# Layer 0 of a four-layer graph network: T2 of the first piece summed by transfers, T1's self-loops on GpSimd, the second half's row statistics on ScalarE

## The chip, the cores and the metric

One core of a Trainium2 chip runs the whole network in one launch. The metric is the device time in microseconds (us); the times shown are a median over runs, and one further execution was profiled.

## The reference

`x` is 2708 x 512 and `adj` 2708 x 2708, both float32. Four layers each take a row-wise layer norm and relu of `x`, multiply by a normalized adjacency, project with a 512 x 512 weight and add the result to `x`. The change lies in layer 0:

```
h = jnp.maximum(_layernorm(x, axis=-1), 0.0)
deg = jnp.sum(adj_matrix, axis=1)
dinv = (deg + 1.0) ** (-0.5)
aug = dinv[:, None] * (adj_matrix + jnp.eye(n, dtype=adj_matrix.dtype)) * dinv[None, :]
x = x + jax.nn.relu(aug @ h @ weight)
```

So layer 0 needs the column-summed degrees, the norm statistics (mean and variance of each row of `x`) and the aggregation with self-loops (the `eye`).

## The kernel before, in words

**Two levels of seven products.** The nodes are cut into 4 quarters of 677 = 5 x 128 + 37. The 5 full tiles of each quarter go through a two-level Strassen-like scheme, the remaining rows through `tails`. At the outer level the features and nodes of `h` form four parts: XA and XB (first half of the nodes, left and right 256 columns) and XC and XD (second half). The adjacency is four quarters y11, y12, y21, y22, each of 2 x 2 blocks of 128 x 5 x 339 float32 (867,840 bytes, shown as 847.5 KB) and two pieces u of 339 columns. Outer product p multiplies a part of `h` by a block sum:

- 1: XA by y11; 2: XC by y21; 3: XC by y22
- 7: XA by T3 = y22 + y12 + I; 6: XA by T2 = T3 + y11 + I
- 4: XD by T4 = T2 + y21; 5: XB by T1 = y12 + y11 + I

XA, XB, XC are overwritten between products (XA becomes XA - XB, then -XD - XA). Below, "p6(1)" is outer product 6 of piece u = 1. In layer 0 the order is p1(0), p1(1), p7(0), p7(1), p6(1), p2(1), p4(1), p6(0), p2(0), p4(0), the tails of two quarters, p5(0), p5(1), two more tails, an epilogue of projections, then p3.

**One outer product of one piece** (`multiply`) is seven inner products of 5 float32 matmuls each, which the trace shows as 10 records, 2.86 us together. Their order on TensorE is pa (factor 1), pb (6), pa again (2), pc (7), pd (5), pc again (4), pd again (3). VectorE makes the sums of blocks (`inner_y`: t1, t2, t4 and, in layer 0, a t3 in a place of its own) and of `h` (`inner_x`), and empties the PSUM banks: pd's second group is accumulated on top of the first, so it may start only after VectorE has read the first one. ScalarE copies pa to `v` before pa's second group.

**Blocks and queues.** 7 block places lie in `obuf`, 3 in `ends` (named `more`), and some early ones in `h` and `agg`. `free` hands them out; a load into a place waits until its last reader is done. Loads go through SP's DMA queue. Stores of block sums to DRAM (`keep_o`, tensors `osum`, read again by the later layers) and accumulating loads go through GpSimd's (POOL's) queue. Each engine works its queue in order. A scheduler decides the order on each engine; `tc.issue_after(i)` keeps instructions behind i.

**Layer 0 before the change.** T3, T2 and T4 are sums on VectorE. `second_sums(0)` makes T2 of the piece u = 0 right after p1(1) and stores it; it is loaded again for p6(0). T1 is a load of y12 on SP's queue and an accumulating load of y11 on POOL's (L697), then `add_loops` on VectorE (L410, three small instructions a block), then a store. The second half's rows of `x` are loaded into `h` (L238) after T3's sums have left that space; `first_stats` takes bn_stats and bn_aggr on VectorE (L202, L203) for 12 tiles; `other_degrees` sums columns, and after its second call `first_h` takes roots and writes the normalized `h` tile by tile on ScalarE (L221). p6(1) needs XA minus XD, and so this.

Of the kernel before, what the change touches and what calls it, by code (L numbers as in the profile page):

```python
# [8 lines left out]
FP = mybir.dt.float32  # L9
# [3 lines left out]
P = 128  # L13
# [8 lines left out]
U = 2  # L22
# [15 lines left out]
def gnn_kernel(  # L38
# [161 lines left out]
    def stats(src, mv):  # L200
        st = small.tile([P, nc.vector.BN_STATS_DIM], FP, tag="st", name="st")
        nc.vector.bn_stats(st, src)  # L202
        nc.vector.bn_aggr(mv, st)  # L203
# [13 lines left out]
        )  # L217
        return b

    def normalized(t, src, scale, shift):  # L220
        nc.scalar.activation(h[:, t, :], src, AF.Relu, bias=shift, scale=scale)  # L221

    def groups(ts):

# [17 lines left out]
    def first_stats(ts):  # L242
        for t in ts:
            stats(h[:, t, :], mv0[:, t, :])

# [68 lines left out]
    def other_degrees(u, ys):  # L314

        if u == 0:
            parts[1, 1] = upool.tile([P, W], FP, tag="s", name="row")
        for b, blocks in ((0, (ys[1], ys[2])), (1, (ys[7],))):
            ps = ps_out.tile([P, W], FP, tag="out", name="dg_ps")
            tl = tail_place(b, u)  # L320
            column_sums(ps, [tl[:, 0], tl[:, 1]], blocks, parts[b, u])
        if u < U - 1:
            return
# [15 lines left out]
    def first_h(columns, looped):  # L339

        ts = list(columns)
        n, t0 = len(ts), ts[0]
        span = slice(t0, t0 + n)
        pd = ps_sm.tile([P, NT], FP, tag="sm", name="pd")
        for s, t in enumerate(ts):
            nc.tensor.matmul(
                pd[:, s : s + 1], columns[t], ones[:, 0:1], start=True, stop=True
            )
        if looped:
            nc.vector.tensor_copy(deg[:, t0 : t0 + looped], pd[:, :looped])  # L350
        if looped < n:
            nc.vector.tensor_scalar(
                deg[:, t0 + looped : t0 + n], pd[:, looped:n], 1.0, None, ALU.add
            )
        rsqrt(dinv[:, span], deg[:, span], n)
        mv = mv0[:, span, :]
        rstd = rstd_of(mv, n)
        nc.vector.tensor_mul(rstd[:, :n], rstd[:, :n], dinv[:, span])
        sh = shift_of(mv, rstd, n)
        for s, t in enumerate(ts):  # L360
            normalized(t, h[:, t, :], rstd[:, s : s + 1], sh[:, s : s + 1])

    def other_roots():

# [39 lines left out]
    def add_loops(blk, u, times):  # L404

        for k in range(KT):
            lo, hi = max(k * P, u * W), min((k + 1) * P, (u + 1) * W)
            if lo < hi:
                o = blk[:, k, lo - u * W : hi - u * W]
                nc.vector.scalar_tensor_tensor(  # L410
                    o, ident[:, lo - k * P : hi - k * P], float(times), o, ALU.mult, ALU.add
                )

    def by_halves(f, *xs):

# [48 lines left out]
            multiply(xs_, inner_y(blks, u, loops), u, dests)  # L464
            free.extend(blks)

    def multiply(xs_, ys, u, dests):


        cu = slice(u * W, (u + 1) * W)  # L470
# [9 lines left out]
        def bank(name):  # L480
            return ps_agg.tile([P, W], FP, tag="agg", name=name)
# [29 lines left out]
        product(pc, 7, True)  # L511
        u3 = upool.tile([P, W], FP, tag="u3", name="u3")
        at_u3.append(nc.vector.tensor_add(u3, u2, pc).ins)  # L513
        pd = bank("pd")
        product(pd, 5, True)
        give(1, 1, pd, u3, ALU.subtract)
# [56 lines left out]
    def first_part_of_both():  # L573
        nc.scalar.copy(agg[:, 0, 1], agg[:, 0, 0])
# [31 lines left out]
    def first_aggregate(epilogue):  # L606
# [42 lines left out]
        def second_sums(u):  # L649
            for (a, b), t2, y in zip(QUAD, blks[u], t3[u]):  # L650
                nc.vector.tensor_add(t2, t2, y)
                keep_o(t2, "t2", a, b, u)

        for (a, b), blk, y in zip(QUAD, t3[0], temps):
            load_plain("y22", a, b, 0, blk)
            load_plain("y12", a, b, 0, y)
# [2 lines left out]
        for (a, b), y in zip(QUAD, temps):  # L659
            load_plain("y12", a, b, 1, y)  # L660
        multiply(xs_, ys, 1, [p1])
        second_sums(0)
        by_halves(nc.vector.tensor_sub, XA, XA, XB)
        xs_ = inner_x(XA)
        ys = inner_y(t3[0], 0, 0, own_t3)
# [8 lines left out]
        ys = inner_y(t3[1], 1, 0, own_t3)  # L674
        with tc.issue_after(at_u3[-1]):
            second_sums(1)
        with tc.issue_after(at_end[-1]):
            first_stats(range(half, NT))
        other_degrees(1, ys)
        multiply(xs_, ys, 1, [p7])  # L680
        first_part_of_both()
        by_halves(minus_sum, XA, XD, XA)
        free += t3[0][:2] + t3[1]

        def among(places):

            for k, f in enumerate(free):
                if any(f is e for e in places):
                    return free.pop(k)
            return free.pop(0)  # L690


        def first_sums(u, places):
            t1 = [among(places) for _ in QUAD]
            for (a, b), blk in zip(QUAD, t1):
                load_plain("y12", a, b, u, blk)
                nc.gpsimd.dma_start(blk, yb[a, b, u], accum_op=ALU.add)  # L697
            with tc.issue_after(at_u3[-1]):
                for (a, b), blk in zip(QUAD, t1):
                    if a == b:  # L700
                        add_loops(blk, u, OUTER[5][2])
                    keep_o(blk, "t1", a, b, u)
            return t1

        for u in reversed(range(U)):
            if u == 1:
                t2 = blks[1]
            else:
                t2 = [among(in_obuf) for _ in QUAD]
                for (a, b), blk in zip(QUAD, t2):  # L710
                    nc.sync.dma_start(blk, osum["t2", a, b, u])
            xs_ = inner_x(XA)
            multiply(xs_, inner_y(t2, u, 0, own_t3), u, [(0, 1, "added")])
            if u == 1:
                other_roots()
                nc.vector.tensor_sub(XB, XB, XD)
            y21 = [among(more) for _ in QUAD]
            for (a, b), blk in zip(QUAD, y21):
                load_plain("y21", a, b, u, blk)
            xs_ = inner_x(XC)  # L720
            multiply(xs_, inner_y(y21, u, 0, own_t3), u, [(0, 0, "added")])
            for (a, b), t4, y in zip(QUAD, t2, y21):
                nc.vector.tensor_add(t4, t4, y)
                keep_o(t4, "t4", a, b, u)
            free += y21
            if u == 0:
                rows = [tail_rows(True, q) for q in (0, 1)]
            xs_ = inner_x(XD)
            multiply(xs_, inner_y(t2, u, 0, own_t3), u, [(1, 0, "as it is")])
            if u == 0:  # L730
                t1 = first_sums(0, more)
            free += t2
        nc.vector.tensor_add(XC, XC, XA)
        tails(True, (0, 1), rows)
        ends_of_sums()
# [402 lines left out]
```

## Time and profile before

| | us |
|---|---|
| median of 3 runs | 2145.58 (2144.49 to 2147.9) |
| the profiled execution's own time | 2147.35 |
| its span | 2145.6 |
| TensorE busy | 2068.6 (96%) |
| VectorE / ScalarE / GpSimd busy | 1438.6 / 384.7 / 173.7 |
| mean granted TensorE clock | 0.989 of full speed |

The span runs from the first to the last instruction. PE is TensorE, DVE VectorE, ACT ScalarE, POOL GpSimd, SP the queue of SyncE. A line number names the line of the kernel that issues the instruction; a helper such as `multiply` gives all its matmuls one line (L475). Layer 0 up to its first epilogue takes the first 374 us of the span; the rest of the program is not touched by the change.

### The profile page before, as it was taken

What the parts mean: (1) busy time and instruction counts of PE and PEld (TensorE: products, weight loads), DVE (VectorE), ACT (ScalarE), POOL (GpSimd) and SP (SyncE); (2) the same over time, 40 slices, a digit from 0 to 9 for tenths busy, and PEclk for the clock granted to TensorE, in tenths of its full rate; (3) what the DMA queues carried; (4) which work ended last, traced back from release to release, by engine and by line L of the source; (5) the groups of instructions that cost most, each with busy time, mean ns of one, the idle gap of its engine ahead of it and who ended that gap; (6) DMA issues with size and microseconds to landing.
All of it is one profiled execution on the core that took longest, in us unless ns stands there. A gap on an engine that the chain in (4) does not pass through costs nothing.

```text
span 2145.6 us, 19944 instructions
## 1 busy us (share of the span) xinstructions
PE 2068.6 (96%) x7310; PEld 1289.0 (60%) x7310; DVE 1438.6 (67%) x2513; ACT 384.7 (18%) x755; POOL 173.7 (8%) x319
## 2 busy tenths in 40 slices
PE   5989979999999999999999999999999999999998
PEld 2555646556666645566664546666677666666664
DVE  3888847667666867777576879968537755666512
ACT  1111000222000010100001121000116534444401
POOL 0000010211000020200001130000001000000001
PEclk9999989999999999999999999999999999999999
DMA  9884695446454443644453656544541233233212
GB/s 351 346 336 154 191 281 189 161 153 211 164 177 167 148 165 137 234 164 156 162 183 123 218 196 211 176 156 156 192 166 72 96 101 103 91 101 100 80 41 64
DMA packets 78720, 358.05 MB, mean 167 GB/s; under 512 B 10540, under 2 KB 14508, under 8 KB 78624
## 3 DMA queue, kind: packets, MB, share of 16 engines
q1 hardware_dynamic: 51104, 250.98, 34.3%
q0 software_dynamic: 27520, 105.82, 14.6%
q8 instruction: 57, 0.93, 0.2%
q14 instruction: 39, 0.32, 0.0%
HBM read 294.61 MB, written 62.15 MB: 166 GB/s over the span
## 4 chain that ended last, share of the span: by engine, by line
PE 62%; issue 20%; DMA 8%; DVE 7%; POOL 2%; ACT 1%; SPq 0%; POOLq 0%; DVEq 0%; ACTq 0%
PE pa L475 13%; PE pc L475 12%; PE pd L475 12%; PE po L754 7%; PE pb L475 6%; PE pe L1045 4%; PE pt L526 3%; PE pg L893 3%; DMA obuf<-in_yb_dram 2%; DMA h<-in_x_dram 1%; PE pt L531 1%; DVE ends L846 1%; POOL ends L761 1%; DMA ends<-xs 1%; DMA osumt<-obuf 1%
## 5 line engine op out<-in xcount | busy, mean ns | idle before, releaser
L1045 PE MATMUL pe<-obuf,h 128*128 128x339 f32 x1280 | 372.9, 448 | 0.0
L475 PE MATMUL pa<-obuf,h 128*128 128x339 f32 x1050 | 324.0, 454 | 13.4 <-DVE h L420 8.5
L1045 PEld LDWEIGHTS pe<-obuf,h 128*128 128x128 f32 x1280 | 241.2, 189 | 126.4 <-issue 10.0
L754 PE MATMUL po<-ends,agg 128*128 128x512 f32 x640 | 281.4, 596 | 2.1 <-ACT ends L774 1.9
L475 PEld LDWEIGHTS pa<-obuf,h 128*128 128x128 f32 x1050 | 200.1, 192 | 121.4 <-issue 9.4
L754 PEld LDWEIGHTS po<-ends,agg 128*128 128x128 f32 x640 | 119.8, 190 | 144.8 <-issue 137.3
L475 PE MATMUL pd<-obuf,s 128*128 128x339 f32 x550 | 169.0, 454 | 13.3 <-DVE agg L492 13.3
L475 PE MATMUL pc<-t,h 128*128 128x339 f32 x560 | 173.8, 457 | 4.4 <-DVE u L513 4.4
L966 ACT ACTIVATE e<-r,nsr 128x339 f32<-128x339 f32 x352 | 170.7, 566 | 28.6 <-DVE obuf L970 11.7
L475 PE MATMUL pb<-t,s 128*128 128x339 f32 x560 | 169.3, 448 | 0.1
L475 PE MATMUL pd<-t,s 128*128 128x339 f32 x560 | 169.2, 448 | 0.0
L503 ACT COPY v<-pa 128x339 f32<-128x339 f32 x56 | 24.6, 440 | 758.4 <-PE pa L475 738.8
L475 PEld LDWEIGHTS pd<-obuf,s 128*128 128x128 f32 x550 | 105.6, 192 | 68.0 <-DVE agg L492 14.3
L475 PEld LDWEIGHTS pc<-t,h 128*128 128x128 f32 x560 | 108.1, 194 | 60.9 <-DVE u L513 6.0
L475 PEld LDWEIGHTS pd<-t,s 128*128 128x128 f32 x560 | 106.0, 189 | 54.2 <-issue 0.5
L475 PEld LDWEIGHTS pb<-t,s 128*128 128x128 f32 x560 | 105.7, 189 | 54.6 <-DVE s L420 0.7
L475 PE MATMUL pc<-obuf,s 128*128 128x339 f32 x450 | 136.1, 448 | 0.0
L475 PEld LDWEIGHTS pc<-obuf,s 128*128 128x128 f32 x450 | 85.3, 189 | 43.6 <-issue 0.5
L450 DVE TENSOR_TENSOR t<-obuf,t 128x1695 f32<-128x1695 f32 x55 | 105.4, 1917 | 0.0
L780 POOL DMA_DIRECT2D xs<-ends x66 | 35.9, 544 | 817.6 <-DVE ends L779 764.8
L451 DVE TENSOR_TENSOR t<-obuf,t 128x1695 f32<-128x1695 f32 x53 | 101.6, 1917 | 0.0
L449 DVE TENSOR_TENSOR t<-obuf 128x1695 f32<-128x1695 f32 x49 | 94.1, 1920 | 9.8 <-DMA obuf<-in_yb_dram 6.6
(247 smaller groups left out, 2184.2 us busy)
## 6 DMA issues: line engine op xcount, KB each, us to landing
obuf<-in_yb_dram SPq DMA_DIRECT2D x131, 847.5 KB, 4.6
obuf<-osumt SPq DMA_DIRECT2D x100, 847.5 KB, 4.5
osumt<-obuf POOLq DMA_DIRECT2D x23, 847.5 KB, 9.0
xs<-ends POOLq DMA_DIRECT2D x66, 256.0 KB, 2.3
ends<-xs POOLq DMA_DIRECT2D x66, 256.0 KB, 3.4
obuf<-in_yt_dram SPq DMA_DIRECT2D x32, 339.0 KB, 3.6
h<-in_yb_dram SPq DMA_DIRECT2D x11, 847.5 KB, 10.0
ends<-in_yb_dram SPq DMA_DIRECT2D x11, 847.5 KB, 6.2
```

Source lines behind the costliest of these rows:

```text
L449: nc.vector.tensor_add(t1, o12, o11)
L450: nc.vector.tensor_add(t2, o22, t1)
L451: at_t4.append(nc.vector.tensor_add(t4, o21, t2).ins)
L475: nc.tensor.matmul(ps, xs_[q][:, k, :], ys[q][:, k, :], start=start and k == 0, stop=k == KT - 1, skip_group_check=not start,)
L503: nc.scalar.copy(v, pa)
L526: nc.tensor.matmul(ps[c], h[:, NF, c * P : (c + 1) * P], tl[:, 0, :], start=start, stop=False)
L531: nc.tensor.matmul(ps[c], h[g, NF + 1, c * P : (c + 1) * P], tl[g, 1, :], start=False, stop=True)
L754: nc.tensor.matmul(po, cs[c], w_sb[:, c, :], start=(c == 0), stop=(c == NC - 1))
L780: nc.gpsimd.dma_start(xs[t], xt)
L893: nc.tensor.matmul(pk, cs[c], wg_sb[:, c, k, :], start=(c == 0), stop=(c == NC - 1))
L966: nc.scalar.activation(e[:, k], row, AF.Exp, bias=nsr[:, t, s : s + 1], scale=1.0)
L1045: nc.tensor.matmul(pe[c], h[:, t, c * P : (c + 1) * P], a, start=(t == 0), stop=False)
```

## The change

- `second_sums(0)` is gone. T2 of u = 0 is made later, in two calls of `second_sums_later` during p2(1) and p4(1): load the stored T3 block, accumulate y11 onto it by a transfer from POOL's queue, add the self-loops of the two diagonal blocks on GpSimd, store.
- T1 takes the same path (`accumulated`): its self-loops move from VectorE to GpSimd, and its blocks are taken in the order (0,0), (0,1), (1,1), (1,0).
- `other_stats` replaces `first_stats` for the second half: two passes of 12 activations of 128 x 512 on ScalarE with an accumulated output (Identity for the sum, Square of mean minus x for the variance), each followed by one small scaling on VectorE.
- `first_h` for the second half is called inside p7(1), ahead of its pd, and not ahead of p7(1)'s first matmul in the program; `normalized` writes half rows (128 x 256), for the second half the right columns (XD) first.
- The copy of agg[:, 0, 0] to agg[:, 0, 1] is a transfer on POOL's queue, no more a ScalarE copy.
- T4's sums and stores stand behind u3 of p6 of the same piece.

```
+    def other_stats(ts):
+        span = slice(ts.start, ts.stop)
+        y = ytp.tile([P, 2, W], FP, tag="yt", name="y").rearrange("p s w -> p (s w)")[:, 0:D]
+        for s, f, mean in ((0, AF.Identity, None), (1, AF.Square, mv0)):
+            for t in ts:
+                nc.scalar.activation(
+                    y, h[:, t, :], f,
+                    bias=0.0 if mean is None else mean[:, t, 0:1],
+                    scale=1.0 if mean is None else -1.0,
+                    accum_out=mv0[:, t, s : s + 1],
+                )
+            nc.vector.tensor_scalar(mv0[:, span, s], mv0[:, span, s], 1.0 / D, None, ALU.mult)
...
-        for s, t in enumerate(ts):
-            normalized(t, h[:, t, :], rstd[:, s : s + 1], sh[:, s : s + 1])
+        fs = slice(0, D // 2), slice(D // 2, D)
+        for f in fs if t0 < half else fs[::-1]:
+            for s, t in enumerate(ts):
+                normalized(t, h[:, t, :], rstd[:, s : s + 1], sh[:, s : s + 1], f)
...
+        def accumulated(blks, key, a_b, u, load):
+            for a, b in a_b:
+                blk = blks[a, b]
+                load(blk, a, b)
+                nc.gpsimd.dma_start(blk, yb[a, b, u], accum_op=ALU.add)
+                if a == b:
+                    add_loops(blk, u, 1, nc.gpsimd)
+                keep_o(blk, key, a, b, u)
...
-        second_sums(0)
...
-        with tc.issue_after(at_end[-1]):
-            first_stats(range(half, NT))
+        other_stats(range(half, NT))
         other_degrees(1, ys)
-        multiply(xs_, ys, 1, [p7])
-        first_part_of_both()
+        multiply(xs_, ys, 1, [p7], other_h)
+        nc.gpsimd.dma_start(agg[:, 0, 1], agg[:, 0, 0])
...
         def first_sums(u, places):
-            t1 = [among(places) for _ in QUAD]
-            for (a, b), blk in zip(QUAD, t1):
-                load_plain("y12", a, b, u, blk)
-                nc.gpsimd.dma_start(blk, yb[a, b, u], accum_op=ALU.add)
-            with tc.issue_after(at_u3[-1]):
-                for (a, b), blk in zip(QUAD, t1):
-                    if a == b:
-                        add_loops(blk, u, OUTER[5][2])
-                    keep_o(blk, "t1", a, b, u)
-            return t1
+            t1 = {ab: among(places) for ab in QUAD}
+            accumulated(
+                t1, "t1", ((0, 0), (0, 1), (1, 1), (1, 0)), u,
+                lambda blk, a, b: load_plain("y12", a, b, u, blk),
+            )
+            return [t1[ab] for ab in QUAD]
+        t2 = {}
+        def second_sums_later(a_b):
+            for ab in a_b:
+                t2[ab] = among(in_obuf)
+            accumulated(
+                t2, "t2", a_b, 0, lambda blk, a, b: nc.sync.dma_start(blk, osum["t3", a, b, 0])
+            )
         for u in reversed(range(U)):
...
+            u3_of_6 = at_u3[-1]
...
+            if u == 1:
+                second_sums_later(QUAD[:2])
             xs_ = inner_x(XC)
             multiply(xs_, inner_y(y21, u, 0, own_t3), u, [(0, 0, "added")])
-            for (a, b), t4, y in zip(QUAD, t2, y21):
-                nc.vector.tensor_add(t4, t4, y)
-                keep_o(t4, "t4", a, b, u)
+            with tc.issue_after(u3_of_6):
+                for (a, b), t4, y in zip(QUAD, ops, y21):
+                    nc.vector.tensor_add(t4, t4, y)
+                    keep_o(t4, "t4", a, b, u)
             free += y21
-            if u == 0:
+            if u == 1:
+                second_sums_later(QUAD[2:])
+            else:
                 rows = [tail_rows(True, q) for q in (0, 1)]
...
```

More of the change, by code (lines that the diff above doesn't have):

```diff
@@ L218, in shift_of, with normalized @@
         return b
-    def normalized(t, src, scale, shift):
-        nc.scalar.activation(h[:, t, :], src, AF.Relu, bias=shift, scale=scale)
+    def normalized(t, src, scale, shift, fs=slice(0, D)):
+        nc.scalar.activation(h[:, t, fs], src[:, fs], AF.Relu, bias=shift, scale=scale)
     def groups(ts):
@@ L321, in other_degrees, with other_h @@
             column_sums(ps, [tl[:, 0], tl[:, 1]], blocks, parts[b, u])
-        if u < U - 1:
-            return
+    def other_h():
         columns = {}
@@ L402, in load_plain, with add_loops @@
         nc.sync.dma_start(blk, yb[j + a, i + b, u])
-    def add_loops(blk, u, times):
+    def add_loops(blk, u, times, engine=None):
         for k in range(KT):
@@ L409, in add_loops @@
                 o = blk[:, k, lo - u * W : hi - u * W]
-                nc.vector.scalar_tensor_tensor(
-                    o, ident[:, lo - k * P : hi - k * P], float(times), o, ALU.mult, ALU.add
-                )
+                i = ident[:, lo - k * P : hi - k * P]
+                if engine is None:
+                    nc.vector.scalar_tensor_tensor(o, i, float(times), o, ALU.mult, ALU.add)
+                else:
+                    assert times == 1
+                    engine.tensor_tensor(o, o, i, ALU.add)
     def by_halves(f, *xs):
@@ L465, in outer_product, with multiply @@
             free.extend(blks)
-    def multiply(xs_, ys, u, dests):
+    def multiply(xs_, ys, u, dests, beside=None):
         cu = slice(u * W, (u + 1) * W)
@@ L513, in multiply @@
         at_u3.append(nc.vector.tensor_add(u3, u2, pc).ins)
+        if beside is not None:
+            beside()
         pd = bank("pd")
@@ L693, in first_sums @@
         def first_sums(u, places):
-            t1 = [among(places) for _ in QUAD]
-            for (a, b), blk in zip(QUAD, t1):
-                load_plain("y12", a, b, u, blk)
-                nc.gpsimd.dma_start(blk, yb[a, b, u], accum_op=ALU.add)
-            with tc.issue_after(at_u3[-1]):
-                for (a, b), blk in zip(QUAD, t1):
-                    if a == b:
-                        add_loops(blk, u, OUTER[5][2])
-                    keep_o(blk, "t1", a, b, u)
-            return t1
-        for u in reversed(range(U)):
[L706 to L711, printed above, removed]
+            t1 = {ab: among(places) for ab in QUAD}
[11 more added lines that the diff above has]
+            )
+        for u in reversed(range(U)):
+            ops = blks[1] if u == 1 else [t2[ab] for ab in QUAD]
             xs_ = inner_x(XA)
-            multiply(xs_, inner_y(t2, u, 0, own_t3), u, [(0, 1, "added")])
+            multiply(xs_, inner_y(ops, u, 0, own_t3), u, [(0, 1, "added")])
+            u3_of_6 = at_u3[-1]
             if u == 1:
@@ L719, in first_aggregate @@
                 load_plain("y21", a, b, u, blk)
+            if u == 1:
+                second_sums_later(QUAD[:2])
             xs_ = inner_x(XC)
             multiply(xs_, inner_y(y21, u, 0, own_t3), u, [(0, 0, "added")])
-            for (a, b), t4, y in zip(QUAD, t2, y21):
-                nc.vector.tensor_add(t4, t4, y)
-                keep_o(t4, "t4", a, b, u)
+            with tc.issue_after(u3_of_6):
+                for (a, b), t4, y in zip(QUAD, ops, y21):
+                    nc.vector.tensor_add(t4, t4, y)
+                    keep_o(t4, "t4", a, b, u)
             free += y21
-            if u == 0:
+            if u == 1:
+                second_sums_later(QUAD[2:])
+            else:
                 rows = [tail_rows(True, q) for q in (0, 1)]
             xs_ = inner_x(XD)
-            multiply(xs_, inner_y(t2, u, 0, own_t3), u, [(1, 0, "as it is")])
+            multiply(xs_, inner_y(ops, u, 0, own_t3), u, [(1, 0, "as it is")])
             if u == 0:
                 t1 = first_sums(0, more)
-            free += t2
+            free += ops
         nc.vector.tensor_add(XC, XC, XA)
```

## The prediction

> **What bounds the kernel now.** The page first: TensorE is busy for 96% of the span, so only its gaps can be won. The table of stretches shows where layer 0 has them.
>
> ```profile
> PE 2068.6 (96%) x7310; PEld 1289.0 (60%) x7310; DVE 1438.6 (67%) x2513; ACT 384.7 (18%) x755; POOL 173.7 (8%) x319
> ```
>
> ```profile
> core 0: us, PE busy (x) PEld busy (x) DVE busy (x) ACT busy (x) POOL busy (x), PEclk, DMA share, GB/s
> 100.00:125.00 25.00, 23.37 (x103) 13.11 (x101) 21.01 (x22) 4.20 (x5) 2.12 (x4) 1.00 1.02 404
> 125.00:150.00 25.00, 21.58 (x89) 14.23 (x89) 23.84 (x50) 1.80 (x6) 2.67 (x5) 0.92 1.00 382
> 150.00:175.00 25.00, 15.94 (x41) 9.55 (x40) 19.45 (x31) 9.25 (x14) 0.53 (x1) 0.74 0.19 70
> 250.00:275.00 25.00, 25.00 (x89) 16.60 (x88) 23.51 (x24) 0.88 (x2) 2.85 (x4) 1.00 0.98 284
> 275.00:300.00 25.00, 12.74 (x41) 8.13 (x40) 7.00 (x14) 0.44 (x1) 6.95 (x10) 0.79 1.02 281
> ```
>
> PE idles in 125 to 175 (call it the head) and in 275 to 300 (the T1 stage). In both the DMA engines are full just before. The chain of waits says what ends the gaps:
>
> ```profile
> 116.26 22.88 DMA h<-in_x_dram
> ...
> 159.54 3.64 ACT h L221 x5
> 163.20 1.50 DVE h L420
> 164.75 5.71 PE pa L475 x10
> ...
> 280.07 13.98 DMA obuf<-in_yb_dram
> ...
> 295.46 1.83 DVE t L449
> 297.29 0.43 DVE agg L492
> 297.77 5.74 PE pd L475 x10
> ```
>
> Head: rows of x issued at 116.3 land at 139.1; bn_stats, roots and twelve activations follow, and p6(1) starts at 164.75, 8.5 us after p7(1) ended. T1: p4(0)'s last group (pd) could start at 285.4. It waits 12.3 us for a PSUM read on VectorE (L492), which stands behind T1's self-loops (L410), which wait for the accumulating load of block (1,1). POOL's timeline shows these loads (L697):
>
> ```profile
> 247.89 0.91 POOL L697 DMA_DIRECT2D ends<-in_yb_dram  x1 [7.74 <-DMA ends<-in_yb_dram]
> 258.07 0.89 POOL L697 DMA_DIRECT2D ends<-in_yb_dram  x1 [1.03 <-DMA ends<-in_yb_dram]
> 267.59 0.89 POOL L697 DMA_DIRECT2D ends<-in_yb_dram  x1 [8.63 <-DMA ends<-in_yb_dram]
> 279.52 1.80 POOL L697 DMA_DIRECT2D obuf<-in_yb_dram  x2
> ```
>
> **What the Trainium skill says.** (1) "TensorE: Matmul & The Clock Gate", Part 1: after about 3.4 us of idling the array runs at half clock for about as long. The trace agrees: ten matmuls take 5.7 us in place of 2.86 after the gaps of 8.5 and 12.3 us, and 3.1 after one of 1.6. (2) "DMA: Bandwidth & Descriptors", Issuing engines are not separate DMA queues: SP's and POOL's transfers share 16 engines. Agrees: 1.0 busy wherever both have work. (3) "GPSIMD Engine Reference", Elementwise: a two-input add takes some 2.6 cycles an element at 1.2 GHz; 0.28 us for 128 columns. No such row in this trace. (4) "SBUF — State Buffer", Who interferes with whom: a VectorE instruction with two SBUF inputs and a GpSimd instruction that reads SBUF exclude each other. Not shown here.
>
> **Prices.** A plain block is 867,840 bytes at the 420 GB/s that full stretches show (84 to 100 us): 2.07 us of all engines. An accumulating one: from 248.8 to 294.1 the engines moved 9 plain blocks (18.6 us) and 5 accumulating ones; less 1.8 us of latency that leaves 24.9, so 5.0 each. Its quickest landing is 7.5 us, its slowest 17.3. Block add 1.83 us, half-size PSUM read 0.42, activation of 128 x 512 0.71 (12 in 8.56, L221). An activation with accumulated output isn't in the trace: from 0.71 to 1.0, I take 0.75. A half-row activation: from the 339- and 512-column rows (566, 797 ns), 0.36. GpSimd add: 0.28 to 1.0 with dispatch and the port, I take 0.4, and up to 1.83 more behind a VectorE add.
>
> **Head.** Removed: four block adds (7.3 us of VectorE) and four stores (8.3 us of DMA) of T2(0), twelve bn pairs (0.67 each, 8.0 us of VectorE), the 2.46 us ScalarE copy. y22(1) overwrites T2(0)'s places, so its four loads no longer wait for stores: in the changed order of SP's queue they follow y12(1) and start near 83 us, not 99.5. T3(1)'s sums then wait for no transfer; the last read of x's place ends near 105.8 us by adding up VectorE's order, and x is issued at 103 and 106 (before 113.9 and 116.3). Still to move then: one y21 block, three T3 stores, x at 3.1 twice, 14.5 us from 101.3: x lands at 114 to 118, not 134 to 139.
>
> Pass 1 on ScalarE is 12 x 0.75: done near 123. Queued behind it stand the two degree copies and p7(1)'s `v`, which pa's second group needs. p7(0) loses its waits and ends near 118 (before 122.6); degrees take 2; p7(1) starts at 120, and `v` is wanted at 126. So pass 1 has 3 us to spare. Pass 2 waits for its mean on VectorE, behind T2(1)'s adds (to 125), then 9 us and two small ScalarE steps: done near 135. p7(1) ends near 142, with 1.8 us for the twelve column matmuls now ahead of pd. The roots' chain waits in VectorE's order for the reads of pd and pc and for two block adds: scales near 142.5. Then 5 half activations (1.9), -XD - XA (1.4): p6(1) at 146. Its pb waits for XB - XD (2.73) and the second half, to 151.5; six groups of 2.86 and half of a cold start give an end at 170. Before: 188.4. **Gain 18**, range 13 to 20 (low end: 1.0 us an activation; x 5 us later costs up to 3).
>
> The agg transfer (1.39 MB, issued near 120, wanted near 160) lies beside it, and the first half's ten half activations take what five whole ones took (10 x 0.36 to 5 x 0.73): nothing.
>
> **T2(0).** The four loads of T3 stand where four loads of T2 stood; new are four accumulations (20 us of DMA) between 135 and 205, where the engines are half busy, and on POOL they wait behind the bg load (for the column matmuls, 134): nothing. But block (1,1) takes the place of a block that p2(1) reads to its end (191). Load 4.6, POOL 0.9 with an accumulation of 7.5 (quiet DMA, 0.5 in this stretch before), three GpSimd adds 1.2, block add 1.83, PSUM read 0.4: VectorE is through at about +17, where p4(1)'s last group wants it at +17.15. **Cost 1**, from 0 to 6 if the accumulation takes 12. p6(0) reads the sums later; covered.
>
> **T1.** Measured from p2(0)'s start (248.2 before). Before: T4's stores at -16, -14, -9 and +8, accumulations from 0, (1,1) landed at +45.9, PE went on at +49.6. In the changed order all four T4 adds stand behind p6(0)'s last PSUM read, so they end at +2.3, +4.6, +8.0, +10.9, and their stores stand ahead of T1's first accumulation on POOL, now at +11.4. The place for (1,1) still comes free at +20. From +2.9 to its landing the engines move 4 accumulating blocks (20) and 13 plain ones (four T4 stores, four y12, three y12 of u = 1, two T1 stores: 26.9): +52 with latency. One accumulation fewer than before (that of u = 1 falls behind), but T4's stores come in. The wait itself stays: in VectorE's order the t3 of p5(0), a reader of (1,1), still stands ahead of the PSUM read that p4(0)'s last group needs. Then adds 1.2, t3 1.83, read 0.4: PE goes on at +55.5. **Loss 6**, from -15 (whole gap and cold start gone) to +15. What follows, tails and p5, has the same order behind it; T1(1)'s chain would end near +79, p5(1) starts near +98: covered.
>
> **Sum.** -18 + 1 + 6 = -11 on the profiled execution's 2147.35 (span 2145.6 and 1.8 around it): 2136.3. That execution lies 1.8 above the median, so I say **2135** for the median.
>
> **Rivals.**
> - *T1's gap shrinks too.* For it: self-loops leave VectorE, and (1,1)'s accumulation no longer stands behind one of u = 1. Against: DMA share 1.02 in that stage. If PE goes on at +40 to +48: 2114 to 2126. Chance 0.27.
> - *The statistics lose what they win.* ScalarE's 24 activations in front of `v`, or x no earlier: p7(1) stalls, 2138 to 2150. Against: 5 us between landing and bn_stats' end now. Chance 0.10.
> - *Slower: POOL's queue becomes a chain.* Each GpSimd add waits for its accumulation, and stores and the next accumulations wait behind it. If adds are also held up by VectorE's two-input adds (1.83 each, three to six in a row), (1,1) is issued at +48 and more. Against: transfers, not issue, fill the stage. The head's 18 are eaten from a landing at +64 on; at +72 to +80: 2150 to 2163. Chance 0.13.
> - *Likeliest*, the sum: 2126 to 2143. Chance 0.50.
>
> **Numbers.** A measurement of this kernel can tell about 0.2% from no change, 4.3 us. The likeliest case gives 0.44 faster and 0.06 same; the second 0.27 faster; the third 0.02 and 0.08; the fourth 0.13 slower. Together 0.73, 0.14, 0.13. Range 2114 to 2150: it leaves out the slower case and a total of both gaps.
>
> **What would show it.** Right: x's rows land near 116, p7(1) ends near 142, p6(1) near 170, ScalarE's 24 activations under 1 us; in the T1 stage PE still idles at pd of p4(0), for 15 to 20 us, with DMA at 1.0. Wrong: pa's second group in p7(1) waiting for ScalarE; PE without a gap in p4(0); GpSimd adds of several us; p4(1) stopping at its end for over 6 us.

## The result, and the profile after

The changed kernel takes **2170.54 us** (median of 4 runs, 2167.51 to 2171.65) against 2145.03 for the kernel before: a ratio of 1.0117, 95% interval 1.0099 to 1.0136. It is slower by 25 us; the forecast was 2135, and 2150 at most. The profiled execution has a span of 2167.8 us (before 2145.6).

TensorE (PE) runs the same 7310 matmuls. It is busy for 7.5 us more, and idle for 14.7 us more (91.7 us of the span, before 77.0):

```profile
PE 2076.1 (96%) x7310; PEld 1293.2 (60%) x7310; DVE 1422.3 (66%) x2475; ACT 406.2 (19%) x824; POOL 185.0 (9%) x342
```

The starts of the block products in TensorE's timeline say where. Each column is the length of a stage in us, from start to start: "head" from p7(0) to p2(1), "T2" p2(1) and p4(1), "T1" p4(0) and the tails after it, then p5(0). p7(0) itself starts at 97 to 103 us in these profiles; the three latest are e4, e5 and e11. Each row is one profiled execution, beside the median of all runs; the ratio is to runs of the kernel before that were taken with them. From the start of p3 on, where no edit changes anything, these executions took 1735.7 to 1739.5 us, so some 4 us of a span can come from there.

| run | head | T2 | T1 | p5(0) | median us | ratio to before (95%) |
|---|---|---|---|---|---|---|
| before | 90.0 | 40.0 | 51.9 | 20.1 | 2145.0 | |
| after | 91.6 | 51.3 | 60.0 | 21.1 | 2170.5 | 1.0117 (1.0099 to 1.0136) |
| e1: statistics alone | 104.9 | 40.0 | 48.6 | 20.1 | 2161.4 | 1.0076 (1.0057 to 1.0095) |
| e2: after, statistics as before | 78.1 | 51.4 | 59.6 | 21.6 | 2159.6 | 1.0064 (1.0045 to 1.0084) |
| e3: after, T2(0) as before | 104.8 | 40.0 | 59.6 | 22.2 | 2174.1 | 1.0134 (1.0113 to 1.0155) |
| e4: after, T1 and T4 as before | 93.4 | 45.9 | 49.0 | 20.1 | 2153.9 | 1.0045 (1.0032 to 1.0058) |
| e5: T2(0) alone | 79.6 | 46.5 | 52.0 | 20.1 | 2143.4 | 0.9994 (0.9984 to 1.0004) |
| e6: after, accumulations first | 92.1 | 48.5 | 62.2 | 21.3 | 2172.8 | 1.0134 (1.0118 to 1.0149) |
| e7: after, pass 1 behind `v` | 82.5 | 51.4 | 59.6 | 21.3 | 2163.4 | 1.0088 (1.0073 to 1.0103) |
| e8: after, T4 as before | 92.9 | 43.6 | 58.2 | 20.1 | 2162.3 | 1.0087 (1.0066 to 1.0108) |
| e9: after, sums bound | 92.1 | 41.9 | 49.0 | 27.4 | 2162.0 | 1.0083 (1.0064 to 1.0102) |
| e10: after, copy on ScalarE | 85.2 | 51.3 | 60.0 | 21.6 | 2165.5 | 1.0101 (1.0084 to 1.0118) |
| e11: e5 with half rows, early degrees | 79.6 | 44.1 | 48.7 | 20.1 | 2142.0 | 0.9987 (0.9980 to 0.9994) |
| e12: e11, three changes of order | 79.6 | 40.0 | 46.9 | 20.1 | 2133.2 | 0.9946 (0.9931 to 0.9960) |
| e13: e8, p5(0)'s sums bound | 92.7 | 45.6 | 42.3 | 28.2 | 2155.6 | 1.0056 (1.0037 to 1.0075) |
| e14: e12, loops bound | 79.6 | 40.0 | 41.3 | 20.1 | 2130.9 | 0.9939 (0.9920 to 0.9959) |
| **e15: e14, roots first** | 70.9 | 40.0 | 40.8 | 20.1 | **2122.3** | **0.9896 (0.9870 to 0.9922)** |
| e16: e15, loops on GpSimd | 70.6 | 40.0 | 43.2 | 28.3 | 2130.7 | 0.9934 (0.9908 to 0.9959) |

From before to after: start 1.3, head 1.6, T2 11.3, T1 8.0, p5(0) 1.0, and -1.0 in all that follows: 22.2, the difference of the spans. Stretches as in the prediction's table, and 300 to 325 (start and end, then busy time and number of instructions of each engine, TensorE's clock, DMA share, GB/s):

```profile
125.00:150.00 25.00, 10.90 (x32) 6.83 (x31) 5.03 (x15) 16.77 (x45) 0.85 (x2) 0.73 0.58 236
150.00:175.00 25.00, 20.55 (x70) 13.29 (x70) 18.74 (x36) 14.57 (x34) 4.06 (x7) 0.80 0.73 186
275.00:300.00 25.00, 21.88 (x77) 14.20 (x75) 18.16 (x19) 0.88 (x2) 3.86 (x8) 1.00 1.03 341
300.00:325.00 25.00, 11.58 (x23) 6.91 (x24) 11.32 (x12) 0.00 (x0) 6.08 (x12) 0.59 0.90 267
```

The head's gap has moved from 150-175 to 125-150, where PE is busy 10.9 of 25 us, VectorE (DVE) only 5.0 and ScalarE (ACT) 16.8: ScalarE is now what the head waits for. The chain of waits in this stretch (start, length, what):

```profile
106.17 30.17 DMA h<-in_x_dram
...
142.34 0.35 ACT v L523
...
142.73 4.97 PE pa L495 x10
```

ScalarE's timeline shows why `v`, a copy of 0.4 us, comes at 142. Brackets hold the idle time before an instruction and what ended it; L252 is pass 1:

```profile
125.41 0.63 ACT L252 ACTIVATE y<-h 128x512 f32<-128x512 f32 x1 [16.62 <-DMA h<-in_x_dram]
...
136.42 0.63 ACT L252 ACTIVATE y<-h 128x512 f32<-128x512 f32 x1 [7.28 <-DMA h<-in_x_dram]
...
142.23 0.45 ACT L523 COPY v<-pa 128x339 f32<-128x339 f32 x1
```

Pass 1 was issued ahead of `v`, and twice waited for rows of x. PE's other waits, in p4(1) (T2) and p4(0) (T1):

```profile
227.82 4.81 PE L495 MATMUL pc<-t,h 128*128 128x339 f32 x10 [2.26 <-DVE u L533]
236.95 5.65 PE L495 MATMUL pd<-obuf,s 128*128 128x339 f32 x10 [4.32 <-DVE agg L512]
...
302.20 5.45 PE L495 MATMUL pc<-t,h 128*128 128x339 f32 x10 [5.32 <-DVE u L533]
318.87 5.64 PE L495 MATMUL pd<-obuf,s 128*128 128x339 f32 x10 [11.22 <-DVE agg L512]
```

Each is a wait for VectorE, and each restart costs more: the ten matmuls behind it take 4.8 to 5.65 us in place of 2.86. That an array that idled runs slower for a while is what "TensorE: Matmul & The Clock Gate", Part 1, of the Trainium skill says, but the length of idling that it gives, about 3.4 us, does not sort these waits: 2.26 us was enough here, and in e8 the same ten matmuls took 3.12 us after a longer wait:

```profile
228.73 3.12 PE L495 MATMUL pc<-t,h 128*128 128x339 f32 x10 [3.22 <-DVE u L533]
```

What VectorE did in T2, and then POOL's queue there and in T1 (the accumulating loads are L681, the stores L415, the self-loops L432):

```profile
226.32 0.19 DVE L570 TENSOR_TENSOR obuf<-obuf,ident 128x32 f32<-128x32 f32 x1 [6.88 <-DMA obuf<-in_yt_dram]
...
234.55 1.93 DVE L472 TENSOR_TENSOR ends<-obuf 128x1695 f32<-128x1695 f32 x1 [6.05 <-POOL obuf L432]
236.39 0.51 DVE L512 TENSOR_TENSOR agg<-pd,u 128x339 f32<-128x339 f32 x1
```

```profile
202.69 0.53 POOL L415 DMA_DIRECT2D osumt<-obuf  x1 [1.72 <-DVE obuf L757]
211.88 0.90 POOL L681 DMA_DIRECT2D obuf<-in_yb_dram  x1 [8.66 <-DMA obuf<-osumt]
223.56 0.55 POOL L415 DMA_DIRECT2D osumt<-obuf  x1 [10.77 <-DMA obuf<-osumt]
224.09 0.92 POOL L681 DMA_DIRECT2D obuf<-in_yb_dram  x1
233.42 1.09 POOL L432 TENSOR_TENSOR obuf<-obuf,ident 128x128 f32<-128x128 f32 x3 [8.41 <-DMA obuf<-in_yb_dram]
...
300.51 0.94 POOL L681 DMA_DIRECT2D obuf<-in_yb_dram  x1
...
315.30 1.13 POOL L432 TENSOR_TENSOR obuf<-obuf,ident 128x128 f32<-128x128 f32 x3 [8.57 <-DMA obuf<-in_yb_dram]
```

In T2 the adds to the tail rows (L570), which wait for a load of these rows, hold up u3 (L533) until 227, and the sum of p6(0) that needs block (1,1) (L472) holds up the PSUM read (L512) until 236. (1,1)'s accumulation is issued at 224.09, right behind a store that POOL issued at 223.56. In T1 (1,1)'s accumulation has landed at 315.3.

### The profile page after: what moved, and what is told of

Its sections match the earlier page's. It is cut to its first block, busy times and chain, and to the rows that moved or that the text cites. A ratio compares the mean times of both kernels' runs of the same rounds, so it can differ in the third digit from the quotient of the medians.

```text
span 2167.8 us, 20020 instructions
## 1 busy us (share of the span) xinstructions
PE 2076.1 (96%) x7310; PEld 1293.2 (60%) x7310; DVE 1422.3 (66%) x2475; ACT 406.2 (19%) x824; POOL 185.0 (9%) x342
## 4 chain that ended last, share of the span: by engine, by line
PE 41%; issue 41%; DMA 8%; DVE 6%; POOL 3%; ACT 1%; SPq 0%; POOLq 0%; ACTq 0%; DVEq 0%
PE pa L495 9%; PE pd L495 8%; PE pc L495 8%; PE po L790 5%; PE pb L495 4%; PE pg L929 3%; PE pt L548 2%; DMA ends<-in_yb_dram 2%; DMA obuf<-in_yb_dram 2%; DMA h<-in_x_dram 1%; DMA ends<-xs 1%; POOL ends L797 1%; DMA obuf<-osumt 1%; PE pt L553 1%; DVE t L471 1%
## 5 line engine op out<-in xcount | busy, mean ns | idle before, releaser
L495 PE MATMUL pa<-obuf,h 128*128 128x339 f32 x1050 | 327.6, 457 | 21.6 <-ACT v L523 14.3
L495 PEld LDWEIGHTS pc<-obuf,s 128*128 128x128 f32 x450 | 85.2, 189 | 43.7 <-issue 0.5
```

Source lines behind the costliest of these rows:

```text
L495: nc.tensor.matmul(ps, xs_[q][:, k, :], ys[q][:, k, :], start=start and k == 0, stop=k == KT - 1, skip_group_check=not start,)
```

## The experiments

**First the parts.** The change has three: the statistics with half rows and the copy as a transfer; T2(0) by accumulating transfers; T1's loops on GpSimd with T4's sums behind u3. The table of stages suggests that each loses by itself; the rivals say that one cause (the late head, or DMA bandwidth) makes the others late.

e1, the first part alone on the kernel before:

```
-            first_stats(range(half, NT))
+        other_stats(range(half, NT))
...
-        multiply(xs_, ys, 1, [p7])
-        first_part_of_both()
+        multiply(xs_, ys, 1, [p7], other_h)
+        nc.gpsimd.dma_start(agg[:, 0, 1], agg[:, 0, 0])
```

> The kernel before with the third part of the change alone: the second half's statistics on ScalarE, its column matmuls ahead of pd in p7(1), half-row activations, the copy of the first part as a transfer. T2(0) and T1 as before. Theory (three separate losses that add up; the head's gain is lost because v stands on ScalarE behind pass 1, and pass 1 waits for x): x is issued near 114 as in the kernel before and lands at 135 to 145, v comes at 145 to 150, p6(1) ends at 190 to 200 (before 188.4): 2147 to 2160 us. Rival (one cause: it is the late head that also makes the T2 and T1 stages late): the same head, and 4 to 8 us more in the T1 stage. Forecast of the prediction for this part: a gain, since VectorE loses the bn pairs: under 2140.

2161.41 us. The head takes 14.9 us more; T2 and T1 lose nothing. x is issued later (111.8 and 114.1) and its second half lands at 145.9, `v` follows at 151.3, p2(1) starts at 202.3, later than I wrote. The part is a loss of 16 us, and it lies in the head.

e2, the changed kernel without the first part:

```
-        other_stats(range(half, NT))
+        with tc.issue_after(at_end[-1]):
+            first_stats(range(half, NT))
...
-        multiply(xs_, ys, 1, [p7], other_h)
-        nc.gpsimd.dma_start(agg[:, 0, 1], agg[:, 0, 0])
+        multiply(xs_, ys, 1, [p7])
+        first_part_of_both()
```

> The changed kernel with the statistics as before (bn_stats on VectorE after p7(1)'s last PSUM read, whole rows, the copy on ScalarE); T2(0) by accumulating transfers and T1's loops on GpSimd stay. Theory: v no longer waits, p7(1) runs through and ends near 147; x lands near 130 since it is issued 10 us earlier than in the kernel before, p6(1) ends at 178 to 186 (before 188.4); then T2 costs 11 and T1 7 as in the changed kernel: 2153 to 2162 us, about 10 under the changed kernel. Rival (one cause, the late head): with the head mended the T2 and T1 stages lose nothing either: under 2145.

2159.63 us. The head is 11.9 us *shorter* than before; T2 loses 11.4 and T1 7.7, about as in the changed kernel. The losses add up; a late head is not their common cause.

e3, the changed kernel with T2(0) made and stored early again, and loaded back:

```
+        second_sums(0)
...
-            ops = blks[1] if u == 1 else [t2[ab] for ab in QUAD]
+                    nc.sync.dma_start(blk, osum["t2", a, b, u])
```

> The changed kernel with T2(0) made as before (added on VectorE behind p1(1), stored, loaded back for p6(0)); statistics on ScalarE and T1's loops on GpSimd stay. Theory: the 11 us in p4(1) go (it takes 20 us again, without a wait at its last groups), the head becomes some us worse (x issued near 114, v near 145 to 150: 0 to 8 us later than in the changed kernel), T1 still costs 7: 2155 to 2168 us. Rival (DMA bandwidth, not POOL's order, makes T2 late): the stall moves to another stage, the time stays at 2168 to 2173.

2174.10 us: slower than I expected, and above the rival's range too. T2 loses nothing now, but the head takes 13.1 us more than in the changed kernel, since x is issued 8 us later and lands up to 31.5 us after that. So the loss did move to another stage, as the rival says, but by way of x and ScalarE: T2(0) by transfers is what brings the head's gain, and without it the statistics cost still more.

e4, the changed kernel with T1's loops (VectorE, old order of blocks) and the T4 sums as before:

```
-                add_loops(blk, u, 1, nc.gpsimd)
+                        add_loops(blk, u, OUTER[5][2])
...
-            with tc.issue_after(u3_of_6):
-                for (a, b), t4, y in zip(QUAD, ops, y21):
+            for (a, b), t4, y in zip(QUAD, ops, y21):
```

> The changed kernel with T1's self-loops on VectorE as before, its order of blocks and issue as before, and the T4 adds at their old place; statistics on ScalarE and T2(0) by transfers stay. Theory: the head (+3) and T2 (+11) stay, PE goes on at +48 to +52 from p2(0)'s start instead of +56.4: 2160 to 2166 us. Rival (GpSimd and the T4 stores don't matter, the stage is filled by transfers that came in late from T2): PE goes on at +55 to +58 as in the changed kernel: 2168 to 2172.

2153.89 us, better than expected: T1 is down to 49.0, and T2 lost 5.9 instead of 11.3 although nothing of T2 was touched. Something of this part also costs T2.

**Then the mechanisms.**

e5, the second part alone on the kernel before:

```
-        second_sums(0)
...
+                second_sums_later(QUAD[:2])
...
+                second_sums_later(QUAD[2:])
```

> The kernel before with the second part alone: T2(0) by accumulating transfers in p2(1) and p4(1), with its self-loops on GpSimd. Statistics, T1 and the T4 adds as before. Theory (four separate terms: no T2(0) on VectorE brings x 10 us earlier and gains 12; T2's chain costs 6 where the T4 stores keep their early place, 11 where they come late; pass 1 ahead of v costs 13 to 15; T1's loops or the late T4 stores cost 7): p6(1) starts at 152 to 154 (before 164.8), p4(1) takes 26, PE goes on at +50 in the T1 stage: 2136 to 2142 us, faster than before. Rival (T2's chain costs its 11 us whatever the T4 stores do): p4(1) takes 31: 2143 to 2147 us.

2143.39 us: no clear difference from before, and by the time alone the rival's. The stages decide for the theory: p4(1) takes 26.5 us (theory 26, rival 31). The part gains 10.4 in the head and gives 6.5 back in T2. (The profiled execution is the slowest of its runs, 2149.48; p7(0) starts 4.5 us later in it than in the profile before.)

e6, the changed kernel with each group's accumulations issued first on POOL:

```
+            for a, b in a_b:
+                load(blks[a, b], a, b)
+                last = nc.gpsimd.dma_start(blks[a, b], yb[a, b, u], accum_op=ALU.add).ins
+            with tc.issue_after(last):
+                for a, b in a_b:
```

> The changed kernel with one change of order on POOL: the accumulating transfers of a group of blocks are issued first, their GpSimd adds and their stores after them, so that no accumulation stands behind a store. Theory (the order on POOL makes (1,1) late in T2): its accumulation is issued when its load has landed, 5 us earlier, and p4(1) takes 25 to 27 us instead of 31.3; T1's stall shrinks by 0 to 5 too: 2160 to 2166 us. Rival (the place of (1,1), free only when p2(1) ends, and the loaded DMA make it late): p4(1) takes 30 to 32 us, 2168 to 2172 us.

2172.77 us, as the rival has it; p4(1) takes 28.5, between the two. (1,1)'s accumulation is issued 32.9 us after p2(1)'s start, in the changed kernel 33.0: its load had only just landed, and the store ahead of it cost nothing. T2 gains 2.8 all the same, and T1 loses 2.2.

e7, the changed kernel with pass 1 bound behind `v` of p7(1):

```
+        with tc.issue_after(at_v[-1]):
+            other_stats(range(half, NT))
```

> The changed kernel with pass 1 of the statistics bound to come after v of p7(1) on ScalarE; nothing else moved. Theory (v waits for pass 1, and pass 1 for x): p7(1) runs without the 14 us wait and ends near 149, pass 2 ends near 148, p6(1) starts at 154 to 159 (changed kernel 167.9): 2157 to 2163 us. Rival (x's landing alone sets the head; v's wait only covers it): p6(1) still starts at 166 to 169: 2168 to 2172 us.

2163.38 us, p6(1) at 158.9, as the theory says. The same 24 activations, on the same late x, cost 9 us less once `v` is not behind them.

e8, the changed kernel with T4's sums and stores at their old place:

```
-            with tc.issue_after(u3_of_6):
-                for (a, b), t4, y in zip(QUAD, ops, y21):
+            for (a, b), t4, y in zip(QUAD, ops, y21):
```

> The changed kernel with the T4 adds and stores at their old place (not behind u3 of outer product 6); T1's self-loops stay on GpSimd, T2 and the statistics too. Theory (it is the late T4 stores, not GpSimd's adds, that collide with T2's loads and with T1's accumulations): p4(1) takes 26 instead of 31.3, PE goes on at +48 to +52 from p2(0)'s start instead of +56.4: 2154 to 2161 us. Rival (GpSimd's adds, in POOL's order between the accumulations, make T1 late): p4(1) takes 26, but PE still goes on at +54 to +58: 2162 to 2167 us.

2162.31 us. In T2 the theory holds: 43.6 instead of 51.3. The load that (1,0) starts with, issued at 199.83 here and at 200.21 in the changed kernel, lets POOL accumulate at 204.69 instead of 211.88, and the load of (1,1), issued at 211.3 in both, lets it go on at 217.63 instead of 223.56. Of T4(1)'s four stores, which POOL issues from 195.9 to 202.7 in the changed kernel, only one is left here at that time (195.87). The 3.6 us that remain are the tail rows' adds. In T1 the rival holds: 58.2. VectorE's timeline shows a cause that neither named:

```profile
303.73 1.93 DVE L472 TENSOR_TENSOR ends<-obuf,ends 128x1695 f32<-128x1695 f32 x1 [20.30 <-POOL obuf L432]
305.57 0.50 DVE L533 TENSOR_TENSOR u<-u,pc 128x339 f32<-128x339 f32 x1
```

VectorE stood 20 us in front of p5(0)'s sum of (1,1), with p4(0)'s u3, ready at 286, behind it. What that sum waited for were GpSimd's adds (POOL L432), so GpSimd is not cleared by this; e13 and e16 come back to it.

e9, the changed kernel with p6(0)'s and p5(0)'s sums bound behind p4's last PSUM read:

```
+                with tc.issue_after(at_end[-1]):
+                    ys = inner_y(ops, u, 0, own_t3)
...
+        with tc.issue_after(last_of_4):
+            ys = inner_y(t1, 0, 0)
```

> The changed kernel, with no work removed: the four block sums of p6(0) are bound to follow p4(1)'s last PSUM read on VectorE, those of p5(0) p4(0)'s. Theory (in T2 and T1 alike PE waits for PSUM reads and for u3, which stand in VectorE's order behind sums of the next product that wait for block (1,1); the block itself is wanted later): p4(0) runs its 20 us without a wait, and p5(0) starts 38 to 43 us after p4(0) (changed kernel 60.0, before 51.9); p4(1) keeps 2 us for the tail rows and p6(0) waits 2 to 4 us for its own sums: 2143 to 2152 us. Rival (the transfers themselves are the limit, the wait only moves to the start of p6(0) and p5(0)): 2163 to 2171 us.

2161.96 us: the sign of the theory, less than half its size. T2 falls to 41.9, with 1.8 us of it moved into p6(0). p4(0) runs its 20 us without a wait, and T1 falls to 49.0, not to 40: the tails' PSUM reads (L588) now stand behind the sum, and p5(0) takes 27.4.

```profile
310.96 1.93 DVE L470 TENSOR_TENSOR t<-obuf,t 128x1695 f32<-128x1695 f32 x1 [12.57 <-POOL obuf L432]
312.81 1.92 DVE L472 TENSOR_TENSOR ends<-obuf,ends 128x1695 f32<-128x1695 f32 x1
314.64 1.75 DVE L588 TENSOR_TENSOR agg<-agg,pt 128x339 f32<-128x339 f32 x4
```

e10, the changed kernel with the copy of the first part on ScalarE:

```
-        nc.gpsimd.dma_start(agg[:, 0, 1], agg[:, 0, 0])
+        first_part_of_both()
```

> The changed kernel with the copy of the first part back on ScalarE in place of the transfer within SBUF. Theory (that transfer, issued at 119 while the second half of x is on its way, is what takes x from 22 to 30 us): x's last rows land at 126 to 130 instead of 136.4, v comes 5 to 9 us earlier, less 0 to 2.5 for the copy itself: 2161 to 2167 us. Rival (the backlog of loads issued before 103 makes x late): x lands at 134 to 138, 2168 to 2173 us.

2165.45 us. x lands 20.0 and 20.9 us after its issue, not 21.6 and 30.2; its last rows are there at 125.5 instead of 136.4, and `v` comes at 133.7, still behind pass 1 and the copy. The transfer was issued 13 us *after* x and yet cost it 9. The medians differ by 5 us, at the edge of what the runs can tell apart; the landing is the firmer number: x's second half took 30.0 to 30.3 us in the changed kernel and in e6 to e9, which have the transfer, and 20.9 to 22.9 in the kernel before, e2, e5 and e10, which do not.

```profile
133.72 0.43 ACT L523 COPY v<-pa 128x339 f32<-128x339 f32 x1
```

**A better order.** e11 is e5 with the column matmuls ahead of pd, half-row activations, and bn_stats no longer bound behind the last PSUM read of the product before:

```
-        with tc.issue_after(at_end[-1]):
-            first_stats(range(half, NT))
+        first_stats(range(half, NT))
...
-        multiply(xs_, ys, 1, [p7])
+        multiply(xs_, ys, 1, [p7], other_h)
...
+        for f in fs if t0 < half else fs[::-1]:
+            for s, t in enumerate(ts):
+                normalized(t, h[:, t, :], rstd[:, s : s + 1], sh[:, s : s + 1], f)
```

> Run e5 (before, with T2(0) by transfers) and from the statistics' part only the column matmuls ahead of pd and the half-row activations; bn_stats stays on VectorE, the copy on ScalarE. Theory (in e5 x is there by 129 and bn_stats is done at 138; what is left of the head's gap is the roots' chain, 10.7 us between block sums on VectorE, and the whole-row activations): p6(1) starts 47 to 52 us after p7(0) (e5 56.4, before 66.6): 2134 to 2140 us. Rival (the statistics' part doesn't pay in any form): 55 to 58 us, 2142 to 2146 us.

2142.01 us, the rival: the head stays at 79.6, p6(1) at 56.4 us after p7(0).

e12 is e11 with three changes of order:

```
-            y21 = [among(more) for _ in QUAD]
+            y21 = [among(more) for _ in range(2 if u == 1 else 4)]
+            if u == 1:
+                y21 = [among(in_obuf) for _ in range(2)] + y21
...
-                second_sums_later(QUAD[2:])
+                second_sums_later(((1, 1), (1, 0)))
...
+                with tc.issue_after(at_u3[-1]):
+                    rows = [tail_rows(True, q) for q in (0, 1)]
```

and p5(0)'s sums bound as in e9. 

> Run e11 with three changes of order: T2(0)'s blocks (1,1) and (1,0) take the places of the y21 blocks that p2(1) is done with first, (1,1) first; the adds to the tail rows are bound behind u3 of p2(0); the sums of p5(0) behind p4(0)'s last PSUM read. Theory (T2's 6.5 us in e5 are the late place of (1,1) and the tail rows' adds ahead of u3; T1's gap is the sums of p5(0) ahead of a PSUM read): p4(1) and p4(0) take 20 us each, p5(0) starts 38 to 43 us after p4(0) (e5 52.0): 2112 to 2124 us. Rival (the transfers are the limit in both stages): waits at the start of p6(0) and p5(0) instead, 2132 to 2140 us.

2133.16 us, within the rival's range. T2 is at 40.0, as the theory says: with T4's stores early, the late place of (1,1) and the tail rows' adds together were its whole loss. T1 still has a wait of 10.4 us at pd, since the loops are on VectorE here and stand where the sums stood (L429, then the read L512). So T1 misses the 38 to 43 us of the theory:

```profile
284.17 0.65 DVE L429 SCALAR_TENSOR_TENSOR obuf<-ident,obuf 128x128 f32<-128x128 f32 x3 [12.25 <-DMA obuf<-in_yb_dram]
...
286.33 0.50 DVE L512 TENSOR_TENSOR agg<-pd,u 128x339 f32<-128x339 f32 x1
```

e13 to e16 settle what was open: GpSimd or VectorE's order in T1, and what bounds the head when x is early.

e13 is e8 with p5(0)'s sums bound, the second half of e9's edit:

```
+        with tc.issue_after(last_of_4):
+            ys = inner_y(t1, 0, 0)
```

> The changed kernel with the T4 adds at their old place (run e8) and the sums of p5(0) bound behind p4(0)'s last PSUM read; T1's self-loops stay on GpSimd. Theory (what T1 still lost in e8, 58.2 us from p4(0) to p5(0) against 51.9 before, is VectorE's order: the sum that waits for block (1,1) stood ahead of u3; GpSimd's adds themselves cost little): p4(0) runs its 20 us, p5(0) starts 40 to 48 us after p4(0): 2144 to 2153 us. Rival (GpSimd's adds in POOL's chain make (1,1) late, and the tails' PSUM reads wait in its place): 54 to 58 us, 2158 to 2163 us.

2155.58 us, between the two: p4(0) and the tails take 42.3, as the theory says, but p5(0) takes 28.2, as in e9. VectorE's order was part of T1's loss; the rest has moved one product on. T1 and p5(0) together take 70.5 us, in e8 78.3, before 72.0.

e14, e12 with T1's loops bound behind p4(0)'s last read:

```
-            with tc.issue_after(at_u3[-1]):
+            with tc.issue_after(at_end[-1] if u == 0 else at_u3[-1]):
                 for (a, b), blk in zip(QUAD, t1):
```

> Run e12 with T1's self-loops, which there are on VectorE as in the kernel before, bound behind p4(0)'s last PSUM read in place of its u3. Theory (the 10 us that PE still waits in p4(0) in e12, and the 12 of the kernel before, are these loops ahead of the read, waiting for (1,1)'s accumulation): p4(0) takes 20 us, p5(0) starts 36 to 40 us after p4(0) (e12 47.0): 2122 to 2128 us. Rival (the wait moves to the tails' PSUM reads): 44 to 47 us, 2130 to 2134 us.

2130.85 us. T1 falls from 46.9 to 41.3, between the two; p4(0) has no wait, and p5(0) keeps its 20.1; PE waits 5.5 us in the tails instead. The time is the rival's: 5.7 us shorter in this stage is 2.3 us in the median. Of the difference, 2.2 us stand in p5(1), where PE now waits for VectorE at pc and pd (22.2 us in place of 20.0).

e15, e14 with p6(1)'s block sums and T4(1)'s bound behind the last step of the roots (`shift_of`):

```
+                with tc.issue_after(at_sh[-1]):
+                    ys = inner_y(ops, u, 0, own_t3)
...
+            with tc.issue_after(at_sh[-1]):
+                for (a, b), t4, y in zip(QUAD, ops, y21):
```

> Run e14 with the block sums of p6(1) and the T4(1) adds bound behind the last step of the second half's roots on VectorE. Theory (the 10 us wait ahead of p6(1) in e11 and e12 is the roots' chain, its small steps standing between five block adds of 1.83 us): p6(1) starts 49 to 53 us after p7(0) (e12 56.4): 2115 to 2123 us. Rival (what ends the wait is the activations or the degrees, the order changes nothing): 55 to 57 us, the time of e14 within 2 us.

**2122.25 us, the fastest of all.** p6(1) starts 49.1 us after p7(0). The roots' chain, from the degrees to the shift, first in e5 and then in e15:

```profile
142.99 0.17 DVE L364 COPY deg<-pd 128x10 f32<-128x10 f32 x1 [1.82 <-PE pd L360]
...
153.66 0.18 DVE L215 SCALAR_TENSOR_TENSOR eps<-mv,hd 128x12 f32<-128x12 f32 x1
```

```profile
138.29 0.17 DVE L366 COPY deg<-pd 128x10 f32<-128x10 f32 x1 [2.53 <-PE pd L362]
...
141.51 0.18 DVE L217 SCALAR_TENSOR_TENSOR eps<-mv,hd 128x12 f32<-128x12 f32 x1
```

The same small steps take 10.7 us among block sums of 1.83 us (9.4 in e14, from which e15 departs) and 3.2 us ahead of them.

e16, e15 with T1's loops on GpSimd in the changed kernel's order of blocks:

```
-                        add_loops(blk, u, OUTER[5][2])
+                    add_loops(blk, u, 1, nc.gpsimd)
```

> Run e15 with T1's self-loops on GpSimd, in the changed kernel's order of blocks. Theory (GpSimd's adds of 0.37 us cost nothing by themselves; with the sums out of the way of the PSUM reads it doesn't matter which engine adds the loops): within 3 us of e15. Rival (each GpSimd add holds POOL until its accumulation has landed, and with it the next accumulation and store): p5(0) starts 5 us or more later after p4(0) than in e15, and the time is 4 to 10 us above e15.

2130.67 us, 8.4 above e15: the rival's time. Its mark did not come where it was set: p5(0) starts only 2.4 us later after p4(0), and then takes 8.2 us more itself. In e15 POOL issues the last three accumulations at 271.0, 272.6 and 290.2, in e16 at 280.0, 289.1 and 298.4, each behind adds or a store that wait for an accumulation. VectorE's sum of (1,1) for u = 1 waits for POOL, and p5(0)'s PSUM reads and u3 stand behind it:

```profile
310.15 1.93 DVE L475 TENSOR_TENSOR obuf<-obuf 128x1695 f32<-128x1695 f32 x1 [5.71 <-POOL obuf L434]
312.00 0.92 DVE L519 TENSOR_TENSOR agg<-pa,agg 128x339 f32<-128x339 f32 x2
312.83 0.49 DVE L536 TENSOR_TENSOR u<-u,pc 128x339 f32<-128x339 f32 x1
```

So the adds' 0.4 us are not the cost; the trace points to what waits behind them in POOL's queue. The edit also brings the changed kernel's order of blocks and puts each store right behind its block, so the 8.4 us are the price of the three together.

## Why the prediction was wrong

- **x's landing: the step that failed first.** The issue at 103 and 106 was right (103.8, 106.2). "14.5 us from 101.3: x lands at 114 to 118" was not: 125.4 and 136.4. Some 9 of the missing us are there without the transfer of the first part as well (20.0 to 22.5 us in e2, e5 and e10). The count was short: the 14.5 us stood for some 6.1 MB, but from 101.3 to 136.4 the engines were full all the time and moved some 14.7 MB (35.1 us at 419 GB/s). POOL's stores at 112.5 and 114.4 and the agg transfer at 119.2, all issued after x, landed before its last rows. The kernel before had shown how long x takes, 18 to 23 us, and I replaced that row by a sum of bytes.
- **"The agg transfer lies beside it: nothing": failed.** e10 prices it at 9 us on x's second half and 5 us in the median.
- **"Pass 1 has 3 us to spare": failed with x.** The price was right (630 ns and a separate read of the accumulator, 186 ns, overlapping to 0.755 a pair; I took 0.75). The second rival named this very queue, ScalarE's activations in front of `v`, at 2138 to 2150 and a chance of 0.10; p7(1) ended at 163.3, not 142. The time lies above even that, since T2 and T1 lost as well. It was under-rated because pass 1 was compared with the forecast landing, not with the measured 18 to 23 us.
- **The head's gain of 18**: a loss of 1.6. What held of it is T2(0)'s removal, 10.4 (e5) to 11.9 (e2).
- **Half rows**: 0.50 us each (24 in 11.91), not 0.36. For the first half "ten halves take what five whole ones took" is off by 1.4: 5.02 against 3.63.
- **T2: "cost 1, from 0 to 6", measured 11.3.** I moved T4(0)'s stores in the T1 step and forgot that the same edit moves T4(1)'s into T2: 7.7 of the 11.3 (e8). The load of (1,1), taken at 4.6, took some 12.2 behind them (211.3 to 223.5). The tail rows' adds, which cost PE 2.3 us in the changed kernel and 4.5 in e5, were not in the sum.
- **T1: "PE goes on at +55.5", measured +56.4; loss 6, measured 8.0.** The wait was where I put it, behind sums of p5(0) that stand ahead of a PSUM read, and here the count of bytes came out: (1,1) landed at +52.9, forecast +52. A second wait, at pc, was missing.
- **The slower rival** (POOL's queue becomes a chain) is a real mechanism: e16 prices it, with the order of blocks and stores that came along, at 8.4 us. Its point of decision, (1,1) landed at +64, was not reached (+52.9), so alone it would not have made the kernel slower.

With the three terms as measured, 1.6 + 11.3 + 8.0, and 2.3 elsewhere less 1.0, the sum gives the 22.2 us between the spans. No range from -15 to +15 on T1 could have covered a head that missed by 20. Two of the signs set for being wrong came: pa's second group in p7(1) waited 14.1 us for ScalarE, and p4(1) stopped near its end, for 2.3 and 4.3 us.

Left open: how a transfer of 1.39 MB, some 3.3 us at 420 GB/s, takes 9 us from x when it is issued after it; and why T2 and T1 are 2 to 3 us shorter in e11 than in e5, with no edit there. The last 3 us of e3, which are not in the stages above, stand behind the start of p3, in the stretch that no edit changes; so do 1.8 of the 4.4 us by which e14 is longer than e12 from p5(1) on.

## What to carry to other kernels

When work moves to an idle engine, ask what is queued behind it there and for which transfer its first instruction waits: an engine that is 19% busy still holds up a 0.4 us copy for 14 us. An instruction that waits for a late block should not stand ahead of a PSUM read or of a chain of small steps on the same engine; bound behind them, with no work removed, such orders, and better places for two blocks, were worth 20 us here (e11 to e15). Take the landing of a transfer from the same transfer in the trace, and not only from the bytes that you count ahead of it: one such count came out here, and the other was short by 11 and 18 us.

## What the hardware showed

- Three GpSimd adds (two of 128 x 128, one of 128 x 83) take 1.1 us alone, some 405 ns for a full one, where the estimate from the cycles an element of "GPSIMD Engine Reference", Elementwise, was 0.28 us. Beside two-input VectorE adds the same three took 3.65 us (e16, beside an add of 2.8) and 5.41 us (e6, lines below). That agrees with the exclusion that "SBUF — State Buffer", Who interferes with whom, describes; the trace before didn't show it.

```profile
167.98 5.41 POOL L432 TENSOR_TENSOR obuf<-obuf,ident 128x128 f32<-128x128 f32 x3
```

```profile
167.69 1.58 DVE L440 SCALAR_TENSOR_TENSOR h<-h 128x1280 f32<-128x1280 f32 x1
169.19 3.03 DVE L748 TENSOR_TENSOR h<-h 128x2560 f32<-128x2560 f32 x1
172.14 1.03 DVE L440 SCALAR_TENSOR_TENSOR s<-h,s 128x640 f32<-128x640 f32 x1
```

- The two transfers of x, 1.31 MB each and issued 2.4 us apart, took 20.0 and 20.9 us without the transfer on POOL's queue that is issued 13 us after them (e10), and 21.6 and 30.2 with it. In the changed kernel POOL's two stores below landed 8.6 to 9.1 us after their issue, and the transfer 10.3 us after its own: transfers of the other queue, issued later, landed first.

```profile
112.53 0.53 POOL L415 DMA_DIRECT2D osumt<-obuf  x1 [5.57 <-DVE obuf L429]
114.37 0.53 POOL L415 DMA_DIRECT2D osumt<-obuf  x1 [1.30 <-DVE obuf L673]
119.16 0.54 POOL L711 DMA_DIRECT2D agg<-agg  x1 [4.26 <-PE pd L495]
```
